# Two conditional attention blocks on one core: maxima over pairs of PSUM banks, centred keys, and tails by half batch

## The chip, the cores and the metric

The kernel runs on one core of a Trainium2 chip. The metric is the device time of one execution in microseconds (us); lower is better. Five engines work side by side and meet only at semaphores: PE (TensorE, matmuls and transposes), DVE (VectorE), ACT (ScalarE), POOL (GpSimd) and SP, which here only issues DMAs. PE's results go to PSUM, which has eight banks of 128 partitions x 512 fp32; DVE and ACT read them there. All else lies in SBUF. "Granted clock" is the share of full speed that PE was given.

## The reference, cut to what matters

Two layers follow each other on x of 8 x 512 x 512 (batch, token, feature), fp32. Both project a normalised x to queries, keys and values, mix, and end in a modulated, gated output projection with a residual. The first layer is linear attention (8 heads of 64); the second is softmax attention (16 heads of 32):

```python
xn = layer_norm(x, norm_w, norm_b)
q = (xn @ q_w + q_b).reshape(Bx, Tx, H, -1)
k = (xn @ k_w + k_b).reshape(Bx, Tx, H, -1)
att = jnp.einsum('bnhl,bmhl->bnmh', q, k)
att = att + (1.0 - mask) * -1000000.0
att = jax.nn.softmax(att, axis=2)
v = ((xn @ v_w + v_b) * src_mask[:, :, None]).reshape(Bx, Tx, H, -1)
y = jnp.einsum('bnmh,bmhl->bnhl', att, v).reshape(Bx, Tx, Dx)
h = layer_norm(y, sb_norm_w, sb_norm_b) * (1.0 + scale) + shift
h = jax.nn.silu(h) @ out_w + out_b
return x + h
```

`scale` and `shift` come from a condition vector. The masks of the inputs are all ones, but the kernel keeps the general form.

## The kernel before

**Precision.** Each projection operand is split into a high and a low part (`hi` is a rounded copy by ACT, `lo` the rest by DVE), and `project` (L927) adds three products of four 128-deep steps: 12 matmuls of 128x512 into one bank.

**An order that is planned.** The kernel is written as generators that record operations; nothing is issued while they run. `Order.place` packs all operations of the kernel onto the engines by a table of durations (`_takes`, L615, with `QUAD`, `ENTER`, `LEAVE` for the ways in which PE's array is used), improves the order by rounds and by random moves (`MOVES`), and `Order.issue` (L590) then writes the instructions out in the order of their planned starts. Almost every instruction therefore has the one source line L604, and groups are told apart by tile names. Each engine runs its queue in order.

**Tiles and waits.** The recording layer has its own `Tile` (L75). `Pool.build` (L158) makes the real tiles, and `Tile.root` (L81) maps a recorded tile to a real one. Before, each of the eight PSUM slots is a real tile of its own, one bank, named mm. The tile framework under it sets the semaphore waits from the accesses to its real tiles; the planner only sets the order. `Banks8` (L219) is the planner's account of free banks.

**First layer, by batch.** `transpose_x` (L907), `l0_k`, `values` (L938), `l0_kn`, `l0_att`, `l0_q`, `l0_y`, `hidden` (L949) and `output` (L979). In `values`, a bank of 12 matmuls is emptied by one DVE instruction (v <- mm, cols, v). The page's span from about 20 to 500 us is this layer; its end overlaps the start of the second.

**Second layer, by group G of four heads (32 groups).** `l1_qk` (L1120) projects keys and queries of the group, splits them and sends them through DRAM to the stacked layout `qst`, `kst` (99 rows: high, low, mask and minus the maximum). `l1_max` (L1140) computes scores once in low precision only to get a row maximum: for each of four chunks of tokens, four matmuls of 32 rows run side by side in the array into four banks ("rows"), and DVE adds the mask row and takes the maximum of each bank with one `tensor_tensor_reduce`, 512 in all. `l1_att` (L1180) computes the exact scores minus the maximum, ACT takes the exponential out of PSUM, `l1_av` (L1200) multiplies with the values in 32-column tiles ("columns") and adds the exponentials up, on POOL or DVE as the planner chooses. The tail of a batch, `l1_y` and `l1_tail` (L1334), runs chunk by chunk inside the next batch's attention: four transposes, then for each 128x128 block one tanh and one scaling by ACT, then DVE's gate and split, the output projection, the residual and the store.

Of the kernel before, what the change touches and what calls it, by code (L numbers as in the profile page):

```python
# [29 lines left out]
QUAD = 430  # L30
# [44 lines left out]
class Tile:  # L75
# [5 lines left out]
    def root(self):  # L81
        if self.tag in self.pool.mixed:
            if self.ap is None:
                tag = f"{self.tag}_{self.slot}"
                self.ap = self.pool.pool.tile(list(self.shape), self.dtype, name=self.name, tag=tag, bufs=1)
            return self.ap
        phys = self.pool.home[self.tag][self.slot or 0]
        if self.pool.dram:
            return phys
        n, rest = self.shape[0], self.shape[1:]  # L90
        ap = phys[0:n, 0 : int(np.prod(rest))]
        if len(rest) > 1:
            names = "abcd"[: len(rest)]
            ap = ap.rearrange(f"p ({' '.join(names)}) -> p {' '.join(names)}", **dict(zip(names, rest)))
        return ap
# [47 lines left out]

class Pool:
# [13 lines left out]
    def build(self):  # L158
        for tag, tiles in self.tiles.items():
# [22 lines left out]
ENTER, LEAVE = 95.0, 150.0  # L182
IDENT, WARM, SPARE_TIME, MARGIN = 2500.0, 21000.0, 240.0, 1000.0
ROUNDS = 8
ROWS = 4
MOVES = (4, 8, 9, 13, 18, 23, 43, 54, 59, 61, 225, 252, 259, 270, 274, 286, 317, 324, 327, 330, 335, 337, 343, 352, 353, 357, 363, 366, 373, 401, 406, 427, 581, 585, 606, 613, 619, 632, 634, 637, 725, 738, 741, 748, 760, 780)
# [32 lines left out]
class Banks8(Room):  # L219
# [3 lines left out]
    def __init__(self, n, tiles):  # L223
        super().__init__(n, tiles)
        self.rows = 0

    def take(self, t):
        self.rows += t.first.mode == "rows"
        return super().take(t)

    def give(self, t):
        self.rows -= t.first.mode == "rows"
        super().give(t)
# [7 lines left out]
    def when(self, o, rows_wait):  # L241

        asked, free = len(o.banks), len(self.free)
        if free < asked:
            return None
        if o.mode != "rows":
            if rows_wait and self.n - free - self.rows + asked > self.n - ROWS:
                return None
            first = self.first()
            if first is not o and free < asked + (len(first.banks) if first else 0):  # L250
                return None
        return self.free[0][0] if asked == 1 else heapq.nsmallest(asked, self.free)[-1][0]


class Order:
# [45 lines left out]
    def add(self, name, calls, takes, late, nbytes=0):  # L301
# [12 lines left out]
        for method, args, kw in calls:  # L314
# [3 lines left out]
            for v in ins:  # L318
# [111 lines left out]
    def pack(self):  # L430
# [26 lines left out]
        def offer(o):  # L457
# [21 lines left out]
            for e in o.takes:  # L479
                heapq.heappush(later[e], (at, o.seq, o))  # L480
# [13 lines left out]
        while done < len(self.ops):  # L494
            pick = self.matmul(now["PE"], later["PE"], waiting, room8)
# [21 lines left out]
            at, e, o = pick  # L517
            o.engine, o.start = e, at
            takes = o.takes[e][1]
            if e == "PE":  # L520
                waiting.remove((o.key, o.seq, o))
                for t in o.banks:
                    take(t)
                if o.mode == "rows":
                    for t, slot in zip(o.banks, sorted(t.slot for t in o.banks)):
                        t.slot = slot
                if at > now[e] + 1.0:
                    o.start += WEIGHTS
                elif o.mode != mode:
                    o.start += LEAVE if o.mode == "full" else ENTER  # L530
# [23 lines left out]
    def matmul(now, later, waiting, room):  # L554

        until = now
        while True:
# [3 lines left out]
            rows_wait, soonest = False, None  # L561
            for _, _, o in waiting:
                at = max(o.ready, room.when(o, rows_wait) or 0.0) if o.banks else o.ready
                if o.banks and room.when(o, rows_wait) is None:
                    at = None
                if at is not None and at <= until:
                    return max(now, at), "PE", o
                rows_wait |= o.mode == "rows"
                if at is not None and (soonest is None or at < soonest):
                    soonest = at  # L570
# [19 lines left out]
    def issue(self, nc, unit):  # L590
# [3 lines left out]
        with self.tc.manual_schedule():  # L594
            for o in sorted(self.ops, key=lambda o: (o.start, o.seq)):
# [5 lines left out]
                for method, args, kw in o.calls:  # L601
                    args = [a.real() if isinstance(a, View) else a for a in args]
# [12 lines left out]
def _takes(engine, method, args, kw):  # L615
# [3 lines left out]
    ins = [a for a in args[1:] if isinstance(a, View) or hasattr(a, "shape")]  # L619
# [9 lines left out]
    if engine == "DVE":  # L629
# [3 lines left out]
        if method in ("scalar_tensor_tensor", "tensor_tensor_reduce"):  # L633
            t += 65.0
# [17 lines left out]
def kernel(ctx: ExitStack, tc: tile.TileContext, x, cond, mask0, mask1, w0, w1, out):  # L652
# [12 lines left out]
    BUFS = {"xc": 4, "xT": 8, "v": 4, "A": 10, "dn": 1, "hl": 2, "yT": 4, "y": 3, "stk": 6, "z": 1, "h": 1}  # L665
# [56 lines left out]
    eg = const.tile([P, 4, 32], F32, name="eg")  # L722
    nc.gpsimd.memset(eg, 0.0)
    for g in range(4):
        nc.gpsimd.memset(eg[:, g, g : g + 1], 1.0)


    mbd = {}

    def prep_mask():  # L730
        mrow = big("y", "mrow", shape=(B, 512))
        nc.sync.dma_start(mrow, masks["L1"])
        nc.gpsimd.tensor_scalar(mrow, mrow, -1.0, MASK, ALU.add, ALU.mult)
# [4 lines left out]
        nc.sync.dma_start(mbd["L1"], mhl.bitcast(F32))  # L738

# [32 lines left out]
    silT = const.tile([P, 8, 32], F32, name="silT")  # L772
# [28 lines left out]
    def prep_emb(l):  # L801
        ssb = []
        for h in range(2):
# [16 lines left out]
            t = const.tile([P, ND, 8], F32, name=f"emb{l}{h}")  # L820
# [86 lines left out]
    def transpose_x(l, b, tag="mm"):  # L907
# [3 lines left out]
        for j in range(ND):  # L911
# [5 lines left out]
            if l == "L0" and b == 0 and j % 2:  # L917
                nc.vector.tensor_scalar(tp, tp, col(l, "ln_w", j), col(l, "ln_b", j), ALU.mult, ALU.add)
            else:
                nc.scalar.activation(tp, tp, AF.Identity, bias=col(l, "ln_b", j), scale=col(l, "ln_w", j))  # L920
            nc.scalar.copy(h, tp)
            nc.vector.tensor_tensor(o, tp, h.bitcast(F32), ALU.subtract)
# [48 lines left out]
    def residuals(l, b, res, chunks):  # L971

        t = big("hl", f"xr{l}{b}{chunks[0]}", F32R, (P, 2, 512)).bitcast(F32)
# [22 lines left out]
    def l0_k(b):  # L996
        mk = big("hl", f"mk{b}", F32R).bitcast(F32)
# [118 lines left out]
    peaks = [const.tile([P, 32], F32, name=f"peak{i}") for i in range(2)]  # L1116
# [3 lines left out]
    def l1_qk(G):  # L1120
        b, g = divmod(G, 4)
        if g == 0:
            t = big("z", f"mrow{b}")
            nc.sync.dma_start(t, masks["L1"][b : b + 1].broadcast_to([P, 512]))
            nc.gpsimd.tensor_scalar(t, t, -1.0, MASK, ALU.add, ALU.mult)
            st["mrow", b] = t
        hl = big("stk", f"hl{G}", F32R, (P, 4, 512))
        for i, k in enumerate(("Wk", "Wq")):
            pp = mm_bank(f"pp{k}{G}")
# [3 lines left out]
            nc.scalar.activation(hi, pp, AF.Identity, bias=bias)  # L1133
            nc.vector.scalar_tensor_tensor(lo, pp, bias, hi.bitcast(F32), ALU.add, ALU.subtract)
# [3 lines left out]
        yield from l1_max(G, hl[:, 2, :], hl[:, 0, :])  # L1138

    def l1_max(G, q, k):  # L1140
# [3 lines left out]
        for c in range(NC):  # L1144
# [5 lines left out]
            for j in range(4):  # L1150
                at = 4 * j + c
                nc.vector.tensor_tensor_reduce(
                    sps[j], sps[j], st["mrow", b], -1.0, 3.0e38, ALU.add, ALU.min,
                    accum_out=peak[:, at : at + 1],
# [3 lines left out]
        nc.vector.transpose(turned, peak)  # L1158
# [21 lines left out]
    def l1_att(G):  # L1180
# [4 lines left out]
        st["yp", G] = bank("a", f"yT{G}")  # L1185
# [14 lines left out]
    def l1_av(G, m):  # L1200
# [3 lines left out]
        es, yp = st.pop(("e", G, m)), st["yp", G]  # L1204
# [26 lines left out]
    def l1_last(G):  # L1231
# [7 lines left out]
        for hf in range(2):  # L1239
            r = slice(256 * hf, 256 * hf + 256)  # L1240
            yp = bank("a", f"yT{G}{hf}")
            acc = []
            for m in range(NC):
# [12 lines left out]
                first = hf == 0 and m == 0  # L1256
                with order.together(1275.0 if first else 430.0):
# [21 lines left out]
            with order.together(430.0):  # L1279
                for j in range(4):  # L1280
                    nc.tensor.matmul(
                        den[32 * j : 32 * j + 32, 0:256], eg[:, g, :],
# [4 lines left out]
    def l1_den(G):  # L1287
# [3 lines left out]
        for j in range(4):  # L1291
            nc.tensor.matmul(den[32 * j : 32 * j + 32, :], eg[:, g, :], acc[j], start=True, stop=True)
# [41 lines left out]
    def l1_tail(b, c):  # L1334
        y = st["L1", "ys", b][c]
        sc, sh = W["L1"]["sc"], W["L1"]["sh"]
        tp = mm_bank(f"hp{b}{c}")
        for j in range(ND):
            nc.tensor.transpose(tp[:, chunk(j)], y[:, chunk(j)], ident)
            yield TR  # L1340
        h = big("h", f"h{b}{c}", F32R, (P, 2, 512))
        f = big("y", f"f{b}{c}")
        for j in range(ND):
            scj, shj = sc[:, j, b : b + 1], sh[:, j, b : b + 1]
            nc.scalar.activation(f[:, chunk(j)], tp[:, chunk(j)], AF.Tanh, bias=shj, scale=scj)
            nc.scalar.activation(tp[:, chunk(j)], tp[:, chunk(j)], AF.Identity, bias=shj, scale=scj)
        nc.vector.scalar_tensor_tensor(tp, f, 1.0, tp, ALU.add, ALU.mult)
        nc.scalar.copy(h[:, 0, :], tp)
        nc.vector.tensor_tensor(h[:, 1, :], tp, h[:, 0, :].bitcast(F32), ALU.subtract)
        st["tail", b] = c  # L1350
        hs = tuple([h[:, o, chunk(j)] for j in range(ND)] for o in range(2))
        xr = big("y", f"xr{b}{c}")
        nc.sync.dma_start(xr, x1[b][chunk(c), :])
        nc.gpsimd.tensor_tensor(xr, xr, W["L1"]["bo"], ALU.add)
        op = mm_bank(f"op{b}{c}")
        yield from project(op, hs, W["L1"]["Wo"], chunk(0), full)
        nc.vector.tensor_tensor(xr, xr, op, ALU.add)
        nc.sync.dma_start(out[b][chunk(c), :], xr)
# [41 lines left out]
    for b in range(B + 1):  # L1400
        last = b == B
        if last:
            first, second = chain(l1_qk(0), l1_qk(1)), chain(l1_qk(2), l1_qk(3))
# [14 lines left out]
        else:  # L1418
# [8 lines left out]
            else:  # L1427
                load_x("L1", 1, x1[1])
                run(mix(values("L1", 0), tail, 13, 12))
# [35 lines left out]
    def behind_front(b):  # L1465
# [8 lines left out]
        for c in range(NC):  # L1474
            yield from l1_tail(b - 1, c)

    def ahead(b):

        n = b + 1
        if b > 0:  # L1480
            yield from values("L1", b)
            yield from l1_qk(4 * b + 3)
        if n < B:
# [108 lines left out]
```

## Time and profile before

| | us |
|---|---|
| median of 3 runs | 1356.1 (1355.79 to 1358.22) |
| the profiled execution, its own time | 1355.07 |
| its span, first to last instruction | 1353.3 |
| PE busy | 1308.4 |
| DVE busy | 1057.2 |
| ACT busy | 725.3 |
| POOL busy | 666.4 |

The mean granted clock was 0.990. The busy shares by slices of the span (tenths) show PE at 9 nearly throughout, DVE at 5 to 7 in the first layer and 7 to 9 in the second. A group line reads: source line, engine, operation, tiles out<-in, shape, count, then busy us, mean ns of one, idle time before and what ended it. The largest group of DVE is the masked maximum:

```
L604 DVE CUSTOM_DVE_ANT_0 mm<-mm,z 128x512 f32<-128x512 f32 x512 | 338.1, 718 | 35.8 <-PE mm L604 35.0
L604 DVE DVE_READ_ACCUMULATOR2_ANT peak<- 128x1 f32 x512 | 71.1, 139 | 0.0
```

### The profile page before, as it was taken

To read this page: it belongs to the slowest core of one execution; us is meant where nothing else is said; L and a number is where in the kernel's file an instruction comes from. 1 tells how busy PE (TensorE), PEld (TensorE's weight loads), DVE (VectorE), ACT (ScalarE), POOL (GpSimd) and SP (SyncE) were. 2 spreads that over 40 slices of the span, in tenths; PEclk is the share of its full clock that TensorE was granted. 3 is DMA by queue.
4 is the path that set the end of the run, shared out by engine and by line. 5 is a ranking of instruction groups with operands and counts; after the bars stand their busy time and mean duration, and the time that the engine had idled before them with its cause. 6 is when DMAs were issued, how large, how long until landed. Compare 5 with 4: busy or idle time off the path is not lost.

```text
span 1353.3 us, 21287 instructions
## 1 busy us (share of the span) xinstructions
PE 1308.4 (97%) x7309; PEld 874.2 (65%) x7309; DVE 1057.2 (78%) x2285; ACT 725.3 (54%) x1366; POOL 666.4 (49%) x764
## 2 busy tenths in 40 slices
PE   9999999999999998999999999999999999999998
PEld 7788788878887876546555565555555555556545
DVE  8576576756657788897788788889789789789796
ACT  4333334433344614755853864863863773683674
POOL 7231523234142523975654547647536565574572
PEclk9999999999999998999999999999999999999999
DMA  7522212112230344664451742653563454446331
GB/s 243 182 73 90 87 33 94 46 57 85 80 101 32 125 142 138 183 164 107 140 159 49 193 143 72 183 163 79 150 167 94 139 147 123 126 133 158 96 86 40
DMA packets 84086, 159.10 MB, mean 118 GB/s; under 512 B 15469, under 2 KB 15593, under 8 KB 83977
## 3 DMA queue, kind: packets, MB, share of 16 engines
q1 hardware_dynamic: 83952, 157.73, 40.1%
q8 instruction: 58, 0.95, 0.3%
q14 instruction: 52, 0.42, 0.1%
q10 hardware_dynamic: 24, 0.01, 0.0%
HBM read 106.81 MB, written 50.89 MB: 117 GB/s over the span
## 4 chain that ended last, share of the span: by engine, by line
PE 46%; DVE 7%; ACT 5%; POOL 3%; issue 2%; POOLq 0%; DVEq 0%; ACTq 0%
PE mm L604 46%; DVE mm L604 3%; POOL A L604 2%; DVE A L604 2%; ACT mm L604 1%; ACT A L604 1%; ACT y L604 1%; ACT xc L604 1%; DVE peak L604 0%; ACT h L604 0%; POOL rsb L604 0%; DVE y L604 0%; DVE hl L604 0%; DVE h L604 0%; DVE stf L604 0%
## 5 line engine op out<-in xcount | busy, mean ns | idle before, releaser
L604 POOL TENSOR_TENSOR A<-A,A 128x512 f32<-128x512 f32 x229 | 316.8, 1403 | 153.7 <-PE mm L604 98.7
L604 DVE CUSTOM_DVE_ANT_0 mm<-mm,z 128x512 f32<-128x512 f32 x512 | 338.1, 718 | 35.8 <-PE mm L604 35.0
L604 ACT ACTIVATE A<-mm 128x512 f32<-128x512 f32 x450 | 248.5, 604 | 143.8 <-PE mm L604 138.7
L604 PE MATMUL mm<-qst,kst 99*128 99x512 f32 (+1 forms) x528 | 192.3, 421 | 8.3 <-DVE peak L604 3.6
L604 PEld LDWEIGHTS mm<-qst,kst 99*128 99x128 f32 x528 | 94.5, 189 | 81.7 <-issue 24.4
L604 PE MATMUL mm<-A,v 128*32 128x512 f32 (+1 forms) x932 | 139.4, 587 | 0.0
L604 DVE TENSOR_TENSOR A<-A,A 128x512 f32<-128x512 f32 x93 | 118.7, 1290 | 21.9 <-PE mm L604 13.1
L604 POOL TENSOR_TENSOR y<-y,bo 128x512 f32<-128x512 f32 x60 | 79.2, 1324 | 109.9 <-DMA y<-in_x 89.3
L604 PE MATMUL mm<-xT,Wkh 128*128 128x512 f32 x384 | 124.3, 413 | 1.8 <-DVE xT L604 0.7
L604 PE MATMUL mm<-Wvh,xT 128*128 128x512 f32 x384 | 115.3, 404 | 0.1
L604 PE MATMUL mm<-ident,xc 128*128 128x128 f32 x512 | 99.0, 281 | 12.0 <-ACT xc L604 3.8
L604 ACT ACTIVATE mm<-mm,cols 128x512 f32<-128x512 f32 x62 | 46.6, 752 | 117.1 <-PE mm L604 117.1
L604 ACT ACTIVATE y<-mm,shL,scL 128x128 f32<-128x128 f32 (+1 forms) x144 | 76.6, 533 | 50.0 <-PE mm L604 37.2
L604 PEld LDWEIGHTS mm<-ident,xc 128*128 128x128 f32 x512 | 65.9, 143 | 45.1 <-ACT xc L604 7.3
L604 PEld LDWEIGHTS mm<-xT,Wkh 128*128 128x128 f32 x384 | 69.6, 188 | 27.1 <-issue 9.1
L604 ACT ACTIVATE hl<-mm,cols 128x512 fp32r<-128x512 f32 x64 | 43.8, 688 | 79.3 <-PE mm L604 52.4
L604 PEld LDWEIGHTS mm<-Wvh,xT 128*128 128x128 f32 x384 | 70.3, 188 | 23.7 <-issue 8.8
L604 PE MATMUL mm<-hl 32*128 32x512 f32 x512 | 75.3, 499 | 6.7 <-DVE hl L604 2.3
L604 PE MATMUL mm<-xT,Wqh 128*128 128x512 f32 x256 | 81.4, 408 | 0.0
L604 ACT ACTIVATE mm<-mm,shL,scL 128x128 f32<-128x128 f32 (+2 forms) x152 | 76.4, 503 | 4.8 <-PE mm L604 4.5
L604 PE MATMUL mm<-Woh,h 128*128 128x512 f32 x224 | 75.2, 435 | 3.7 <-DVE h L604 2.2
L604 PEld LDWEIGHTS mm<-hl 32*128 32x128 f32 x512 | 29.1, 183 | 72.3 <-issue 29.8
(204 smaller groups left out, 2732.8 us busy)
## 6 DMA issues: line engine op xcount, KB each, us to landing
kst<-dWk SPq DMA_DIRECT2D x96, 256.0 KB
qst<-dWq SPq DMA_DIRECT2D x96, 256.0 KB
dWk<-hl SPq DMA_DIRECT2D x32, 512.0 KB
dWq<-hl SPq DMA_DIRECT2D x32, 512.0 KB
xc<-in_x SPq DMA_DIRECT2D x32, 256.0 KB
y<-in_x SPq DMA_DIRECT2D x32, 256.0 KB
x<-y SPq DMA_DIRECT2D x32, 256.0 KB
xc<-x SPq DMA_DIRECT2D x32, 256.0 KB
```

The costliest lines, as they stand in the source:

```text
L604: getattr(engine, method)(*args, **kw)
```

## The change

1. **PSUM as four tiles of two banks.** `Pool.build` makes four real tiles of 128x1024 (named pair), and `root` gives a recorded bank one half. A view `Banks` spans both halves. The planner's account of banks (`Banks8.choose`) takes two whole pairs for a "rows" group and prefers banks whose neighbour is taken for others.
2. **Maxima without a mask.** Keys are centred over the kept tokens and set to zero where masked, once, in `l1_qk`; `l1_max` then reduces two banks with one `tensor_reduce`, 256 in all. The maxima of a group are recorded within the next group's projections (`st["late"]`).
3. **Tails by half batch**, as in the code below: scaling out of PSUM into SBUF in 128x256 blocks, one tanh over 512 columns.
4. **Banks emptied into SBUF** in the second layer's `transpose_x` too, for batches after the first.
5. **Planner.** A table of gaps between the ways of using the array in place of `ENTER` and `LEAVE`, `QUAD` 235 for 430, a lean toward neighbouring "rows" and "columns" groups, additions that DVE takes only later (`YIELD`), other `MOVES`, other numbers of buffers (`hl` 3, `y` 4, `h` gone).
6. **Order of stages.** Values of the second layer's first batch move ahead of its third key group; residuals of the last batch are loaded earlier.

```diff
@@ Tile.root, Banks, Pool.build
+        if self.pool.psum:
+            base = 512 * (self.slot % 2)
+            return self.pool.pairs[self.slot // 2][0 : self.shape[0], base : base + self.shape[1]]
...
+class Banks:
+    def __init__(self, views):
+        self.parts, self.shape = views, (P, len(views), 512)
+    def real(self):
+        pool, (a, b) = self.parts[0].tile.pool, [v.tile.slot for v in self.parts]
+        assert a % 2 == 0 and b == a + 1
+        return pool.pairs[a // 2].rearrange("p (n c) -> p n c", c=512)
...
     def build(self):
+        if self.psum:
+            self.pairs = [self.pool.tile([P, 1024], F32, name=f"pair{i}", tag=f"pair{i}", bufs=1) for i in range(4)]
+            return
...
@@ l1_qk
-            hi, lo = hl[:, 2 * i, :], hl[:, 2 * i + 1, :]
...
+            if k == "Wk":
+                kept = st["kept", b]
+                mean = sm.tile([P, 2], F32, name=f"mean{G}", tag="mean")
+                km = big("y", f"km{G}")
+                nc.vector.scalar_tensor_tensor(
+                    km, pp, bias, kept, ALU.add, ALU.mult, accum_out=mean[:, 0:1]
+                )
+                nc.vector.tensor_scalar(mean[:, 1:2], mean[:, 0:1], minus[:, b : b + 1], None, ALU.mult)
+                nc.vector.scalar_tensor_tensor(km, kept, mean[:, 1:2], km, ALU.mult, ALU.add)
+                nc.scalar.copy(hi, km)
+                nc.vector.tensor_tensor(lo, km, hi.bitcast(F32), ALU.subtract)
...
-        yield from l1_max(G, hl[:, 2, :], hl[:, 0, :])
+        yield from st.pop("late", iter(()))
+        st["late"] = l1_max(G, hl[:, 2, :], hl[:, 0, :])
...
@@ l1_max
-            for j in range(4):
-                at = 4 * j + c
-                nc.vector.tensor_tensor_reduce(
-                    sps[j], sps[j], st["mrow", b], -1.0, 3.0e38, ALU.add, ALU.min,
-                    accum_out=peak[:, at : at + 1],
-                )
+            for u in range(2):
+                nc.vector.tensor_reduce(
+                    peak[:, 2 * u : 2 * u + 2, c], Banks(sps[2 * u : 2 * u + 2]), AX.X, ALU.max, negate=True
+                )
...
@@ l1_tail, now for a half batch of two chunks
+            z, f2 = (big("y", f"{p}{b}{hf}{u}").rearrange("p (w n) -> p w n", w=2) for p in "zf")
+            for w in range(2):
+                j = 2 * u + w
+                nc.scalar.activation(
+                    z[:, w, :], tp[:, 256 * w : 256 * w + 256], AF.Identity,
+                    bias=sh[:, j, b : b + 1], scale=sc[:, j, b : b + 1],
+                )
+            nc.scalar.activation(f2, z, AF.Tanh)
+            nc.vector.scalar_tensor_tensor(z, f2, 1.0, z, ALU.add, ALU.mult)
+            nc.scalar.copy(hh[:, js, :], z)
+            nc.vector.tensor_tensor(hl[:, js, :], z, hh[:, js, :].bitcast(F32), ALU.subtract)
...
```

## The prediction

> **What bounds the kernel now.** I read the page's busy table first, then stretches of the span, then single instructions.
>
> ```profile
> PE 1308.4 (97%) x7309; PEld 874.2 (65%) x7309; DVE 1057.2 (78%) x2285; ACT 725.3 (54%) x1366; POOL 666.4 (49%) x764
> ...
> PEclk9999999999999998999999999999999999999999
> ```
>
> PE is the bound: 97% busy, 45 us idle in 1353.3. DVE, at 78%, isn't. The stretches (busy us of each engine, instructions in brackets, then the granted clock) separate the two layers:
>
> ```profile
> 100.00:300.00 200.00, 200.00 (x1264) 161.68 (x1263) 131.81 (x269) 75.38 (x132) 65.03 (x107) 1.00 0.21 69
> 500.00:560.00 60.00, 55.12 (x256) 36.22 (x256) 54.84 (x130) 30.33 (x52) 31.55 (x35) 0.91 0.49 157
> 560.00:760.00 200.00, 193.02 (x1021) 110.09 (x1020) 160.07 (x363) 123.72 (x241) 122.20 (x117) 0.99 0.52 141
> 760.00:960.00 200.00, 192.67 (x1028) 112.17 (x1026) 173.17 (x388) 127.45 (x244) 122.14 (x121) 1.00 0.50 133
> 960.00:1160.00 200.00, 191.50 (x1000) 108.78 (x1001) 167.67 (x386) 121.44 (x231) 110.79 (x106) 0.97 0.45 127
> 1160.00:1340.00 180.00, 170.64 (x949) 97.54 (x950) 148.38 (x300) 119.83 (x242) 105.84 (x102) 0.99 0.42 113
> ```
>
> In the first layer (100:300) PE has no idle time at all. In the second it loses 7.0 + 7.3 + 8.5 + 9.4 = 32 us from 560 on, with DVE at 80 to 87%. That, and no more, is what a lighter DVE can give back.
>
> Why the first layer runs without a gap is seen in the order of time at 199 us (start, duration, engine, operation):
>
> ```profile
> 199.60 0.74 DVE L604 SCALAR_TENSOR_TENSOR v<-mm,cols,v 128x512 f32<-128x512 f32 x1
> ...
> 199.96 1.09 PE L604 MATMUL mm<-Wvl,xhL 128*128 128x512 f32 x4
> ...
> 200.89 0.86 PE L604 MATMUL mm<-Wvh,xlL 128*128 128x512 f32 x3
> ```
>
> DVE empties one bank for 0.74 us while PE accumulates the next projection into another; four matmuls from 199.96 to 200.89 make 0.23 us each. PE meets a reader only when it wants that reader's own bank back, many matmuls later. Where it can't go on, the trace shows the price of a whole round trip:
>
> ```profile
> 844.95 0.51 PE L604 MATMUL mm<-hl 32*128 32x512 f32 x4
> ...
> 845.52 0.70 DVE L604 CUSTOM_DVE_ANT_0 mm<-mm,z 128x512 f32<-128x512 f32 x1 [1.33 <-PE mm L604]
> ...
> 846.13 0.14 DVE L604 DVE_READ_ACCUMULATOR2_ANT peak<- 128x1 f32 x1
> ...
> 846.33 0.55 PE L604 MATMUL mm<-ident,yT 128*128 128x128 f32 x3 [0.86 <-DVE peak L604]
> ```
>
> The reader starts 0.06 us after the matmul's end (845.46), PE 0.06 us after the reader's. PE stood for 0.86 us.
>
> **The change, part by part.** *Maxima.* 512 sums with a mask (pitch 0.65 us, from 846.13 to 846.78, accumulator read included: 333 us of DVE) become 256 reductions over 1024 elements. No row has that shape. Upper bound, two 512-wide reductions:
>
> ```profile
> L604 DVE TENSOR_REDUCE km<-mm 128x1 f32<-128x512 f32 x32 | 22.1, 690 | 1.4
> L604 DVE TENSOR_TENSOR xc<-mm,rd 128x256 f32<-128x256 f32 x64 | 26.9, 424 | 2.0
> ```
>
> 1.38 us; lower bound, the slope from 256 elements (0.42) to 512 (0.69): 0.69 + 2 x 0.26 = 1.21. I take 1.21, the nearer in kind (one instruction, one start): 310 us, 23 saved (bounds: 23 saved, 20 lost).
>
> *Centred keys.* Per group, DVE's one 0.74 us instruction becomes an accumulating one (0.74 + 0.14 for the accumulator read), a tiny scaling (0.22, the 128x8 row), a scalar-tensor-tensor and a subtraction in SBUF (0.70 each by PSUM rows; 1.29 by the A<-A,A row): 2.5 to 3.7 us. 32 times +1.8 to +2.9 is +56 to +94; I take 56. It delays the maxima behind it on DVE, but these now go one group later ("late"), so it meets PE only through banks.
>
> *Sums of exponentials.* In the built order DVE keeps 54 of its 114 additions; 60 x 1.29 = 78 us leave it and 60 x 1.40 = 84 us go to POOL, from 49% to 55%: hidden. *Tails by half batch, banks emptied into SBUF.* ACT loses 224 instructions of 0.52 us and gains 56 of 0.58 and 28 of 0.63: -66 us, at 54% busy, hidden. SP has three DMAs more (608 against 605), all in the preparation: hidden. DVE in all: -23 + 56 - 78 = -45 (bounds -45 and +13); it is off PE's path in the first layer, and of the 32 us of idle time in the second I take 20 back (bounds 0 and 32).
>
> *PE's own work* stays: 6191 matmuls against 6180 (11 fillers more, in waits). The switches between whole-array and 32-row or 32-column matmuls fall from 513 to 492; at 0.09 us each (full-width pitch 0.33 before a switch, 0.23 without): -2 us.
>
> *Banks.* This part decides. The eight one-bank PSUM tiles become four two-bank tiles; root() hands out halves. The planner still thinks in single banks, but in the built order the waits are set by the two-bank tile. The same place, a value projection, in both (first the kernel before, then the changed one):
>
> ```
> 116 Matmult mm_207<-Wvl_0_111,xT_150 128x512
> 117 Matmult mm_207<-Wvh_0_104,xT_145 128x512
> ...
> 107 Matmult pair_206<-Wvh_0_102,xT_143 128x512
> 108 Matmult pair_206<-Wvh_0_104,xT_145 128x512
> 109 Matmult pair_206<-Wvh_0_106,xT_147 128x512 [waits DVE_49]
> ```
>
> That wait, in the middle of an accumulation, is for the DVE instruction that empties the other half. The reader in turn waits for the last matmul placed before it, also one into this half. So PE stops for a round trip where it now flows. Following each wait of PE to the reader and from there to the matmul which that waits for, 589 of PE's 1303 waits on DVE and ACT name a reader of the other half only; before there is none. What PE has to do between the two matmuls (at 0.23 us per full matmul) is the cover:
>
> - first layer: 120 waits (75 on DVE, 45 on ACT) with one matmul of cover, 54 (42, 12) with 0.3 to 0.9 us, 71 with more;
> - second layer: 59 (17, 42) with one matmul, 80 (10, 70) with 0.3 to 0.9, 205 with more.
>
> A round trip is a matmul's 0.40, 0.06 to the reader less rounding (0.04 to 0.06), the reader's 0.74 (DVE) or 0.60 (ACT, row A<-mm, 604 ns), and 0.05: 1.24 or 1.09. Behind one matmul 1.24 - 0.23 = 1.01 or 0.86 is left open; behind 0.6 us, 0.64 or 0.49; beyond 0.9 next to nothing. First layer: 75 x 1.01 + 45 x 0.86 + 42 x 0.64 + 12 x 0.49 = 76 + 39 + 27 + 6 = 148. Second: 17 + 36 + 6 + 34 = 93. Together 241 us. Trips that overlap are counted twice; queues before a reader aren't counted. Low end: the one-matmul waits alone, 168. High end: each reader also finds its engine in another instruction (DVE 66% busy, 0.37 us left on average: 0.24 x 313 = 76), 317.
>
> Readers wait for each other too: 98 DVE reads name an ACT read of the other half, 79 ACT reads a DVE one. Nothing to 0.6 us each on the path, 0 to 106 us; most stand off it, I take 15.
>
> The Trainium skill speaks for the change here: "PSUM — Partial Sum Buffer", in its summary of rules for kernel authors, asks for semaphores by bank and says to read a different bank while matmuls run, which is what the trace of before does at 199.60. By that rule alone the neighbour costs nothing and the sum would be some 22 us below the span; the waits in the built order are wider than the rule.
>
> *Clock.* 500:560 shows the granted clock at 0.91 where PE idles 4.9 us of 60; over the whole span a mean of 0.990 (13.5 us of clock) goes with 45 us of idle time, 0.3 us lost per idle one, and in 760:960 none with 7.3. For 241 us: 0 to 72; short gaps between dense matmuls are nearest to 760:960, I take 24. The skill's "TensorE: Matmul & The Clock Gate", Part 1, says the gate halves after an idle window of about 3.4 us; gaps of 1 us alone would then cost nothing, and 24 would fall out of the sum.
>
> **Sum.** 1353.3 + 241 + 15 + 24 - 20 - 2 = 1611. The profiled run stands at 1355.1 against its span of 1353.3, the median at 1356.1, so +2.8: 1614 us.
>
> **Rivals.** (1) *Wider waits that cost nothing* (faster): readers finish before PE gets there. For it: DVE and ACT are lighter. Against: 179 waits have a single matmul before them, and no reader in the trace takes under 0.4 us. Time: 1356 - 20 - 2 = 1334, down to 1322 with all 32 us. Chance 0.06. (2) *Half hidden*: overlapping trips share their stall and PE, once late, finds readers done: 120 us instead of 241, no clock loss: 1356 + 120 + 15 - 22 = 1469. Chance 0.14. (3) *Clock collapse*: half clock through much of the first layer, as at 510 us: +72 and the upper 317: 1356 + 317 + 72 + 40 (of the readers' 106) - 22 = 1763. Chance 0.08. (4) *DVE becomes the bound* through keys and reductions at their upper prices: 1057 + 13 = 1070 is far below any of these spans; 0.01, inside the others. The side changes where the open round trips come to under 37 us, 22 gained and 15 lost; the one-matmul waits of the first layer alone are three times that.
>
> **Numbers.** Forecast 0.71, hence 1614. Its own ends are 1356 + 168 - 32 = 1492 and 1356 + 317 + 15 + 24 - 2 = 1710; half of (2) and most of (3) and (1) stay out: range 1480 to 1710. Faster by over 0.2% (what a measurement of this kernel can tell from no change): 0.06; within it 0.01; slower 0.93.
>
> **What would show it.** PE's busy share falls to 78 to 86%, in the first layer most of all: the first maxima of the second layer, at some 500 us before, come near 650. PE's waits on DVE and ACT grow from under 150 us to over 300, with the readers v<-pair and y<-pair among them. The two-bank reduction should read 1.2 to 1.4 us. It is wrong if PE still fills 100:300 without a gap.

## The result, and the profile after

The changed kernel takes 1696.9 us (median of 4 runs, 1685.6 to 1703.2) against 1356.3: 1.250 times as long, 95% interval 1.243 to 1.257. The profiled execution took 1703.2 us, its span is 1701.4, 348 us more than before.

The page's busy table and clock line of the changed kernel:

```profile
PE 1440.2 (85%) x7331; PEld 892.1 (52%) x7331; DVE 1034.5 (61%) x1587; ACT 700.5 (41%) x1226; POOL 745.0 (44%) x818
...
PEclk9999989789899999999989999999999997999988
```

Every engine but PE has less to do or a smaller share, and PE, with nearly the same matmuls (6191 for 6180), is idle for 1701.4 - 1440.2 = 261 us in place of 45. The stretches (busy us of PE, PEld, DVE, ACT, POOL, then granted clock, DMA share, GB/s) show where:

```profile
100.00:300.00 200.00, 157.80 (x820) 111.58 (x819) 94.41 (x195) 56.94 (x96) 42.66 (x67) 0.94 0.17 57
300.00:500.00 200.00, 160.28 (x816) 114.92 (x815) 82.52 (x159) 47.91 (x82) 44.98 (x72) 0.87 0.12 40
...
760.00:960.00 200.00, 179.54 (x883) 96.28 (x884) 147.14 (x188) 95.67 (x169) 113.78 (x105) 0.97 0.41 111
```

The first layer, which had no gap in 100:300 and started 1264 matmuls there, starts 820. The first matmul of the second layer's maxima comes at 684.3 us in the trace, before at 477.5. DVE is at 47 and 41% in the two stretches of the first layer: it isn't too busy. PE stands still while DVE or ACT carries out a single instruction. The order of time of the changed kernel shows how (weight loads and POOL left out):

```profile
128.58 0.71 PE L665 MATMUL pair<-Wqh,xhL 128*128 128x512 f32 x2
...
129.33 0.75 ACT L665 ACTIVATE pair<-pair,cols 128x512 f32<-128x512 f32 x1 [12.54 <-PE pair L665]
...
130.13 0.97 PE L665 MATMUL pair<-Wql,xhL 128*128 128x512 f32 x3 [0.84 <-ACT pair L665]
...
132.17 0.63 PE L665 MATMUL pair<-Wqh,xlL 128*128 128x512 f32 x2
132.91 0.69 DVE L665 TENSOR_TENSOR xT<-pair,xT 128x512 fp32r<-128x512 f32 x1 [3.10 <-PE pair L665]
133.65 0.73 PE L665 MATMUL pair<-Wqh,xlL 128*128 128x512 f32 x2 [0.85 <-DVE xT L665]
```

One query projection, in one bank, is stopped after two matmuls while ACT works on a transposed x in another bank, and later while DVE reads another. Each stop leaves PE idle for 0.84 or 0.85 us; the prediction's example from before had 0.86.

In the view of waits (engine, awaited, total us, times, longest; PE's and its weight loads' waits on DVE and ACT) no reader stands out after the first; they come from every stage of the kernel:

```profile
PEld pair L665 <- ACT A L665: 153.9, 198, 2.1
...
PE pair L665 <- ACT A L665: 65.2, 118, 1.2
...
PEld pair L665 <- ACT y L665: 32.2, 41, 1.4
...
PEld pair L665 <- DVE y L665: 27.8, 32, 1.8
...
PEld pair L665 <- ACT pair L665: 22.6, 20, 1.6
...
PEld pair L665 <- DVE xc L665: 21.0, 23, 1.2
```

Before matmuls, PE's idle time that DVE or ACT ended grew from 36 us to 251; before weight loads, which overlap with matmuls, from 150 to 489.

The clock fell too: a mean of 0.954 over 1701 us is 78 us lost, against 13.5 before.

### The profile page after: what moved, and what is told of

Same layout as the page of the kernel before. It is cut to its first block, busy times and chain, and to the rows that moved or that the text cites. A ratio compares the mean times of both kernels' runs of the same rounds, so it can differ in the third digit from the quotient of the medians.

```text
span 1701.4 us, 20590 instructions
## 1 busy us (share of the span) xinstructions
PE 1440.2 (85%) x7331; PEld 892.1 (52%) x7331; DVE 1034.5 (61%) x1587; ACT 700.5 (41%) x1226; POOL 745.0 (44%) x818
## 4 chain that ended last, share of the span: by engine, by line
PE 57%; ACT 10%; DVE 10%; issue 3%; POOL 1%; DMA 1%; SPq 0%; ACTq 0%; DVEq 0%; POOLq 0%
PE pair L665 56%; ACT A L665 5%; DVE peak L665 2%; ACT y L665 1%; DVE pair L665 1%; DVE y L665 1%; DVE A L665 1%; ACT pair L665 1%; POOL A L665 1%; DVE xc L665 1%; DVE hl L665 1%; ACT hl L665 1%; DVE v L665 1%; DMA y<-x 0%; ACT yT L665 0%
## 5 line engine op out<-in xcount | busy, mean ns | idle before, releaser
L665 ACT ACTIVATE A<-pair 128x512 f32<-128x512 f32 x450 | 252.6, 599 | 260.7 <-PE pair L665 237.3
L665 DVE TENSOR_REDUCE peak<-pair 128x2 f32<-128x1024 f32 x256 | 301.2, 1217 | 67.1 <-PE pair L665 66.2
L665 PE MATMUL pair<-qst,kst 99*128 99x512 f32 (+1 forms) x528 | 204.2, 435 | 28.8 <-ACT A L665 17.7
L665 PEld LDWEIGHTS pair<-qst,kst 99*128 99x128 f32 x528 | 97.3, 194 | 122.2 <-ACT A L665 52.6
L665 PE MATMUL pair<-A,v 128*32 128x512 f32 (+1 forms) x932 | 144.4, 615 | 4.8 <-ACT A L665 3.6
L665 PE MATMUL pair<-xT,Wkh 128*128 128x512 f32 x384 | 125.6, 435 | 17.9 <-ACT A L665 6.4
L665 PE MATMUL pair<-Wvh,xT 128*128 128x512 f32 x384 | 124.3, 421 | 19.1 <-ACT A L665 5.4
L665 PE MATMUL pair<-ident,xc 128*128 128x128 f32 x512 | 94.3, 292 | 14.2 <-ACT pair L665 2.4
L665 PE MATMUL pair<-Woh,hl 128*128 128x512 f32 x224 | 79.5, 442 | 13.2 <-ACT A L665 4.8
L665 PE MATMUL pair<-xT,Wqh 128*128 128x512 f32 x256 | 78.5, 414 | 7.2 <-ACT A L665 3.5
```

The costliest lines, as they stand in the source:

```text
L665: getattr(engine, method)(*args, **kw)
```

## The experiments

Times of all runs stand against the kernel before on the same chip. "By classes" is the prediction's sum: waits for a reader of the other half, counted in the built order by the PE work that covers them.

**e1_one_bank: the same order, one-bank waits.** The planner still plans two-bank reductions; only when the order is written out is each bank a tile of its own and each reduction two.

```diff
+PAIRED = 0
...
-            self.pairs = [self.pool.tile([P, 1024], F32, name=f"pair{i}", tag=f"pair{i}", bufs=1) for i in range(4)]
...
+            self.ones = {
+                i: self.pool.tile([P, 512], F32, name=f"one{i}", tag=f"one{i}", bufs=1) for i in range(PAIRED, 8)
+            }
...
+        for u, part in enumerate(banks.parts):
+            yield method, [args[0][:, u : u + 1], part, *args[2:]], kw
```

> The changed kernel's planned order, to the instruction, with eight one-bank PSUM tiles; each two-bank reduction is issued as two one-bank reductions. Theory A (the waits of the two-bank tiles are the whole loss): PE names no reader of another bank any more; 1300 to 1350 us, first maxima of the second layer at 470 to 490 us as before, half clock under 40 us in all, DVE some 256 x 0.16 = 40 us busier than in the changed kernel. Rival B (the new order, the centred keys or the tails cost the time): stays above 1500 us, since all of these are still there.

1352.5 us, ratio 0.9967 (0.9955 to 0.9979). The first maxima come at 481.6 us. The page and two stretches of this kernel:

```profile
PE 1315.6 (97%) x7331; PEld 882.9 (65%) x7331; DVE 1048.9 (77%) x1843; ACT 685.9 (51%) x1226; POOL 751.7 (56%) x818
```

```profile
100.00:300.00 200.00, 200.00 (x1273) 164.25 (x1272) 137.01 (x275) 76.89 (x136) 63.23 (x104) 1.00 0.20 68
...
760.00:960.00 200.00, 192.88 (x1000) 112.90 (x996) 168.10 (x279) 112.70 (x200) 134.59 (x128) 0.97 0.49 130
```

The order, the centred keys, the tails and the planner's table are all still there, and PE is full again. The tiles of two banks, with the joint reductions that they allow, cost 344 us (1696.9 - 1352.5), which is the whole loss; all the rest of the change together is worth some 4 us (1356.8 - 1352.5). DVE is 14 us busier than in the changed kernel (1048.9 - 1034.5), not the 40 expected: the joint reductions saved little. The time lies 2.5 us above the range that was expected: theory A's cause held, its guess of a further gain did not. Rival B fell.

**e2_before_pairs: the kernel before, with two-bank tiles.** Order and arithmetic unchanged.

```diff
+        if self.pool.psum:
+            base = 512 * (self.slot % 2)
+            return self.pool.pairs[self.slot // 2][0 : self.shape[0], base : base + self.shape[1]]
...
```

> The kernel before, order and arithmetic unchanged, only its eight PSUM tiles become halves of four two-bank tiles. Its built order then has 643 waits for a reader of the other half; by the classes of the prediction 96 us in the first layer and 87 in the second, 183 in all. In the changed kernel 240 us by classes came to 341 measured, 1.42 times. Theory A: 1356 + 183 x 1.42 = 1616 us (1560 to 1670), first maxima near 477 + 136 = 613 us. Rival B: within 20 us of 1356.

1729.1 us, ratio 1.275 (1.273 to 1.277): the loss appears in a kernel that has nothing else of the change. First maxima at 582.4 us, 105 later (96 by classes). The total is 59 us over the upper expectation, all in the second layer, where the clock fell as well:

```profile
100.00:300.00 200.00, 180.18 (x1052) 134.90 (x1053) 113.14 (x235) 63.79 (x112) 53.24 (x88) 1.00 0.19 63
...
560.00:760.00 200.00, 166.69 (x748) 96.80 (x748) 138.77 (x319) 79.87 (x135) 85.73 (x84) 0.91 0.40 113
```

**e3_half_pairs and e6_high_pairs: the changed kernel's order, half of the banks as two-bank tiles.** e3 keeps slots 0 to 3 in two-bank tiles, e6 slots 4 to 7; reductions in one-bank slots are split as in e1. The lines are those of e3, with `PAIRED = 4`; e6 has `<` in place of `>=`.

```diff
+            if self.slot >= PAIRED:
+                return self.pool.ones[self.slot][0 : self.shape[0], 0 : self.shape[1]]
...
```

> The changed kernel's planned order again, with slots 0 to 3 as two two-bank tiles (two-bank reductions kept there) and slots 4 to 7 as one-bank tiles (reductions there split). 193 waits for the other half are left of 589, 65 us by classes of 240. Theory A: 65 x 1.42 = 92 us above e1_one_bank (60 to 130). A rival in which the loss comes from the clock gate tipping over as a whole: no clock loss here, so at most 65 above. Rival B: as the changed kernel, near 1697.

> The complement of e3_half_pairs: the changed kernel's order, slots 4 to 7 as two two-bank tiles, slots 0 to 3 as one-bank tiles with split reductions. 412 waits for the other half, 174 us by classes (114 in the first layer). Theory A with the ratio of e3 (75 us for 65): 1353 + 174 x 1.15 = 1553 us without clock loss. If the loss of clock comes with dense waits, the first layer shows half clock again (40 us and more, half of it lost) and the time is 1575 to 1630, near the changed kernel's 1697 less e3's 75. If the clock loss needs both halves, 1553 or less.

e3: 1428.1 us, ratio 1.053 (1.051 to 1.055), 76 us above e1 for 65 by classes, with no half clock in its first layer. e6: 1604.2, ratio 1.181 (1.177 to 1.186), 252 above e1 for 174, inside the range expected where clock is lost in the first layer. Together 328 us against the 344 of the whole: the parts add up. The stretch 100:300 of e3:

```profile
100.00:300.00 200.00, 183.27 (x1108) 144.62 (x1106) 123.84 (x255) 68.35 (x122) 57.34 (x94) 1.00 0.19 65
```

The same stretch of e6, and its page:

```profile
100.00:300.00 200.00, 165.17 (x946) 122.17 (x946) 102.13 (x209) 59.73 (x102) 51.06 (x81) 0.97 0.19 63
```

```profile
PE 1399.0 (87%) x7331; PEld 882.8 (55%) x7331; DVE 1044.8 (65%) x1788; ACT 695.8 (43%) x1226; POOL 747.2 (47%) x818
```

Four kernels can be laid side by side in the first layer, where nothing else of the change acts. Lateness is the start of the first maxima less that of e1 (of the kernel before for e2); half clock is the time in the trace's clock record before it, of which half is lost:

| | by classes, us | late, us | half clock, us | late without clock, by classes |
|---|---|---|---|---|
| e3_half_pairs | 35 | 43.8 | 0 | 1.25 |
| e2_before_pairs | 96 | 104.9 | 10 | 1.04 |
| e6_high_pairs | 114 | 145.6 | 27 | 1.16 |
| changed kernel | 148 | 202.7 | 75 | 1.12 |

The last column is lateness less half of the half clock, divided by the class sum. In the first layer the count of waits carries the size within a quarter; the clock is a second term that grows faster than the first. In the second layer the same reckoning falls shorter: what is late there, less the change in lost clock, is some 1.3 times the class sum in e3 and the changed kernel, 1.4 in e6 and 2.1 in e2.

**e4_rows_low and e5_rows_low_one: can the two-bank reductions be kept?** Planned anew, with the maxima held to slots 0 to 3; e5 is e4's order to the instruction with one-bank tiles.

```diff
-            pairs = [(max(now, free[i][0], free[i + 1][0]), i) for i in (0, 2, 4, 6) if i in free and i + 1 in free]
+            pairs = [(max(now, free[i][0], free[i + 1][0]), i) for i in (0, 2) if i in free and i + 1 in free]
...
```

> As e3_half_pairs, but planned anew with the maxima held to slots 0 to 3, so that all 256 two-bank reductions are kept. 229 waits for the other half, 99 us by classes. Theory A: 99 x 1.42 = 140 us above e1_one_bank, plus what two fixed pairs cost the order (0 to 40): 1440 to 1530 us. Rival B: near 1697.

> The planned order of e4_rows_low to the instruction, with eight one-bank tiles and split reductions. e4 came out at 1629, some 275 us above e1_one_bank where 140 were expected. Theory A (waits for the other half, and the clock they cost): this order alone costs next to nothing, 1345 to 1390 us, half clock under 60 us. Rival C (maxima held to four fixed banks starve PE): 1450 us or more.

e4: 1628.8 us, ratio 1.201 (1.199 to 1.203), 99 us over the upper end of its expectation. e5: 1506.8, ratio 1.110 (1.105 to 1.114). So rival C held for more than half of it: this order alone costs 154 us over e1, and the waits for the other half only 122 (99 by classes). In e5's waits on other engines the maxima themselves come first now; in e1 they stood for 27 us, behind the exponentials (A) with 41:

```profile
PEld one L673 <- issue: 179.3, 396, 1.7
PEld one L673 <- DVE peak L673: 85.5, 204, 2.0
PEld one L673 <- ACT A L673: 41.0, 85, 1.5
```

By the edit, four score matmuls need all four slots empty, that is, the last reduction done; each engine runs its queue in order, so they hold PE until then. In e5's second layer the clock fell without one wait for another half (mean 0.947, 80 us lost).

**e7_free_banks and e9_more_moves: the parts without the pairs, planned for that.** One reduction per bank is recorded, a rows group takes any four free banks, and the planner's random moves were drawn anew; e9 has 13 moves more.

```diff
-            for u in range(2):
-                nc.vector.tensor_reduce(
-                    peak[:, 2 * u : 2 * u + 2, c], Banks(sps[2 * u : 2 * u + 2]), AX.X, ALU.max, negate=True
-                )
+            for j in range(4):
+                nc.vector.tensor_reduce(peak[:, j, c : c + 1], sps[j], AX.X, ALU.max, negate=True)
...
```

> All parts of the change but the two-bank tiles, planned anew for one-bank maxima: 512 reductions of one bank each, a rows group may take any four free banks, and the random moves of the planner drawn anew. Theory A: PE is the bound again and has 30 us idle and some 20 us of clock to gain: 1300 to 1345 us. Rival D (DVE, some 1050 us busy, sets the pace in the second layer): 1345 to 1360, as e1_one_bank.

> e7_free_banks with 13 further random moves of the planner, nothing else. Theory A (PE is the bound, idle time left in the second layer): 1305 to 1322 us. If the order is no longer what holds it: 1320, as e7.

e7: 1319.8 us, ratio 0.971 (0.969 to 0.974). e9: 1319.2, ratio 0.972 (0.971 to 0.974). Both beat both kernels. From e7's page and second layer:

```profile
PE 1285.0 (97%) x7315; PEld 868.7 (66%) x7315; DVE 1048.8 (80%) x1829; ACT 685.6 (52%) x1226; POOL 776.5 (59%) x832
```

```profile
760.00:960.00 200.00, 195.37 (x1053) 114.24 (x1053) 175.10 (x286) 120.77 (x215) 147.91 (x136) 1.00 0.52 140
```

DVE does as much as in e1 (1048.8 and 1048.9 us) and sets no pace; PE starts 1053 matmuls where it started 1000 in e1 and 1028 before, at full clock. Rival D fell. The 13 further moves of e9 add nothing; its 1319.2 us lies in both expectations and doesn't decide between them. Nor is e7's gain split: e7 plans for single banks and also carries 27 random moves, where the changed kernel and e1 carry 3 and the kernel before 46. How much of the 33 us between e1 and e7 comes from the moves alone, no run shows.

**e8_plain_keys: without centred keys.** As e7, with keys and masked maxima as before, each group's maxima recorded within the group.

```diff
-                nc.vector.tensor_reduce(peak[:, j, c : c + 1], sps[j], AX.X, ALU.max, negate=True)
+                nc.vector.tensor_tensor_reduce(
+                    sps[j], sps[j], st["mrow", b], -1.0, 3.0e38, ALU.add, ALU.min,
+                    accum_out=peak[:, j, c : c + 1],
+                )
...
```

> As e7_free_banks, but keys as in the kernel before (split straight out of PSUM, not centred, not masked), maxima as before (mask row added and maximum taken bank by bank, 512 in all) and recorded within their own group; planner, tails and one-bank tiles as in e7, random moves drawn over as many. DVE is lighter by the key work, 56 us by the prediction, and by 512 x (680 - 650) ns = 15 us at the maxima. Theory E (e7's gain comes from lighter DVE work and the tails): as fast as e7 or faster, 1300 to 1325 us. Rival F (it comes from the centred keys' maxima being taken one group later, and from the order that this allows): 1335 to 1365 us, although DVE is lighter.

1337.4 us, ratio 0.986 (0.983 to 0.989): slower than e7, though DVE has 1001 us to e7's 1049. That is the low edge of rival F, and speaks against theory E. It isn't settled: recording the maxima one group later, the arithmetic and the planner's moves (15 in e8, 27 in e7) changed together.

## Why the prediction was right, point by point

**The waits of the two-bank tiles.** The mechanism, its place and its side were right: e1 takes it away from the changed kernel, e2 puts it into the kernel before, e3 and e6 divide it. The forecast of a first layer that is no longer full, of first maxima near 650 us (684.3 came) and of a PE share of 78 to 86% (85) held, and PE's waits on DVE and ACT grew as told. The median, 1696.9, lies near the upper end of the range, because two terms were too small, the stops and the clock, and nothing made up for them. PE's idle time grew by 216 us, and its busy time by 132; about 65 of that is clock, and the other 67 I put to the stops (an estimate), since a matmul at a stop is on record for some 0.40 us in place of a pitch of 0.23. So the stops cost some 216 + 67 = 283, where 241 + 15 - 20 - 2 = 234 were forecast: 49 too little. The prediction said that queues before a reader weren't counted; the table's ratios of 1.04 to 1.25 may be what this leaves open, but no run here takes those queues away. For e2's second layer the count was off by far more (266 us late against 87 by classes and some 80 of clock), and that part is not explained.

**The clock.** This is the mis-sized term: 24 us forecast, 78 - 13.5 = 65 measured. The view taken as nearest, 760:960 with no loss, was the wrong one; 500:560 was nearer. The Trainium skill's rule in "TensorE: Matmul & The Clock Gate", Part 1, that an idle window of about 3.4 us halves the clock, would have made this term nothing for gaps of 0.85 us. The runs say otherwise: in the changed kernel's 300:500 the clock stood at 0.87 with 40 us of gaps, none longer than 1.0 us. In e3, with 17 us of gaps in 100:300, it stayed at 1.00, so a rate per idle microsecond doesn't describe it either. In the first layer, what does is PE's idle time within one stretch of 3.41 us, the step in which the traces' clock records change. Of the 16 falls to half clock in the four kernels of the table, 15 come right after a stretch with 1.57 us idle or more (one after 1.45), each time made up of two stops; of the 609 other stretches at full clock (from 40 us on) only 4 hold as much. In e3 none holds more than 1.54. One such stretch of the changed kernel and the next:

```profile
148.21:151.62 3.41, 1.84 (x9) 0.92 (x7) 1.24 (x2) 1.56 (x3) 0.11 (x1) 1.00 0.00 0
151.62:155.03 3.41, 2.56 (x6) 1.19 (x7) 1.07 (x2) 0.30 (x1) 0.11 (x1) 0.50 0.00 0
```

At half clock a single stop per stretch was enough to stay there: it lasted after 0.68 us idle or more, and ended after 0.49 or less. So the term grows with stops that fall close together, not with their sum. In the second layer this doesn't hold: e5's falls there come after as little as 0.36 us idle, and the runs don't say why.

**The rule for the neighbouring bank.** The Trainium skill's "PSUM — Partial Sum Buffer", in its summary of rules for kernel authors, allows reading one bank while matmuls fill another, and e1 agrees, at 200.00 us busy of 200. It was no rival to the waits, because these come from the tile that the program declares.

**The lighter engines.** The two-bank reduction was forecast at 1.21 us:

```profile
L665 DVE TENSOR_REDUCE peak<-pair 128x2 f32<-128x1024 f32 x256 | 301.2, 1217 | 67.1 <-PE pair L665 66.2
...
L665 DVE SCALAR_TENSOR_TENSOR y<-z,mean,y 128x512 f32<-128x512 f32 x32 | 31.1, 973 | 1.0
```

1217 ns came. DVE in all fell by 23 us, where 45 were forecast. The centring in SBUF takes 0.97 where 0.70 was taken, inside its bounds and hidden, as forecast. ACT's relief was overrated: the 0.52 us for each of the 224 instructions removed was a mean over 128x128 and 128x512 blocks, and the 128x128 ones took 0.46 and 0.43. That is some 17 of the 41 us between the 66 forecast and the 25 by which ACT fell; the rest isn't traced. At 41% busy this cost nothing. The 20 us taken back in the second layer can't be seen in the changed kernel. In e1, without the stops, the whole rest of the change is worth some 4 us, so 20 was too much, though e7 shows that some 37 are there for an order planned without pairs and with more moves.

**The rivals.** "Wider waits that cost nothing" is out by e1 and e2, "half hidden" (1469 us) by the time itself. Half of "clock collapse" came true: its clock term (72) was near the 65 measured, its stops (317 + 40 - 22 = 335) over the 283.

**Slips in the working that didn't bear on the side.** The upper bound of DVE's added work is 20 + 94 - 78 = 36 us by the prediction's own terms, not 13. The side changes where the open round trips come to 22 - 15 = 7 us, not 37. And there were readers under 0.4 us: in the kernel before, 64 reciprocals of 128x4 read PSUM in 0.17 us each.

## What to carry to other kernels

Before joining buffers so that one instruction can read two of them, ask what the join does to every other user of either buffer: here 256 instructions gained and each of the 6191 matmuls came under a wider wait. A planner that keeps its own account of banks must share it with whatever sets the waits; the built order, read for waits in the middle of an accumulation, shows the mismatch without a run. Count such waits by the work that covers them and price each with one whole round trip from the trace; that was good to a quarter in the first layer, and too low by 1.3 to 2.1 times in the second. Where PE must stop, keep the stops apart: in this first layer two whole ones in one stretch of 3.41 us cost clock as well.

## What the runs showed of the hardware that had not been expected

The clock fell under many short gaps: 75 us at half clock in the first layer of the changed kernel, none in that of e3, with the same matmuls and gaps of the same kind but fewer. What counted was how much of two gaps fell into one stretch of 3.41 us, as above.

The new splits, the centring and the gate, DVE instructions with two 128x512 operands in SBUF, took 1.03 to 1.24 us on average in e7, with POOL at 59%, and 0.80 to 0.97 in the changed kernel, with POOL at 44%, against 0.68 to 0.69 for plain sums and differences of that size with one operand in PSUM. It goes with POOL: in the changed kernel the split hl<-y,hl took 0.68 us for the 12 that ran while POOL stood idle and 1.14 on average for the 25 with POOL busy from end to end, while y<-y,pair, which reads PSUM, took 0.685 in both cases (14 and 27).
